# A Restormer block on one core: new due times, GpSimd's results due later, and the weights' preparation moved

## The chip, the cores and the metric

The kernel runs on 1 core of one Trainium2 chip. The metric is device time in microseconds (us). The kernel before takes 4175.92 us (median of 3 runs, 4175.73 to 4176.47). The engines are called PE (matmuls; PEld is its loading of weights), DVE (vector), ACT (activations), POOL (GpSimd) and SP (which only starts DMAs here).

## What is computed

A transformer block on an image batch `x` of 16 x 128 channels x 96 x 96, in float32: channel attention with a residual, then a convolutional feed-forward with a residual.

```
x_hwc = x.transpose(0, 2, 3, 1)
xn1 = _layernorm(x_hwc, ln1_w, ln1_b)
attn_out = _attention(xn1, wq, wk, wv, wp)      # 8 heads, 16 x 16 channel attention per head
x = x + attn_out.transpose(0, 3, 1, 2)
x_hwc = x.transpose(0, 2, 3, 1)
xn2 = _layernorm(x_hwc, ln2_w, ln2_b).transpose(0, 3, 1, 2)
x = x + _ffn(xn2, w_in, w_dw, w_out)            # 1x1 to 512, depthwise 3x3, gelu, 1x1 back to 128
```

In `_attention`, q and k are normalised over the pixels of the image, their product gives a 16 x 16 matrix per head, and its softmax is applied to v. So the first norm and a Gram matrix of a whole image must be finished before the attention's small matrices exist, and these must exist before the second half of the image can begin.

## The kernel before

**Tiling.** An image has 9216 pixels. They are handled in bands of 12 rows (1152 columns of a 128-partition tile), units of 4 rows (384 columns), and quads of 4 blocks of 128 pixels. The hidden 512 channels are four chunks of 128.

**The stages of an image.** First norm ("a"): a band of x is loaded, PE transposes a quad (`forth`, L609), DVE takes its statistics (L616), POOL computes variance plus epsilon (L623) and its power -0.5 (L627), ACT scales the quad into `zT` (L663; DVE does half in the first image, L650), PE accumulates the Gram matrix (L677) and transposes back (`back`, L714), and ACT copies the result into a padded tile `xn` (`place`, L720). Then the attention: about 14 short steps that go back and forth between PE, DVE, POOL and ACT, and end in one 128 x 128 matrix per image. Second norm ("b"): PE multiplies the matrix with `xn` (`mix`, L566), the residual is added (L572, or L575 and a DMA that adds x, L578), and the same steps as in the first norm follow, with a shift by DVE (L631) and ACT's L667 and L718. Feed-forward: PE makes a hidden chunk (L899), ACT copies it to a padded tile (L904), and the depthwise 3 x 3 filter runs in three ways: one chunk of some bands as nine matmuls on PE (L967, gelu at L973); otherwise DVE adds most of the taps (L917), and for two or three taps ACT makes a product (L912) that POOL's DMAs add (L921). Gelu is L925. PE's L990 goes back to 128 channels, DVE adds the residual (L997), SP stores (L1001).

**The order of the work.** `Plan` collects every piece of work with its engine, its cost in ns, a place on a common axis, what it reads and writes, and how long its result takes to reach another engine. `Plan.order` then walks through all of it by a list schedule: an engine that is idle takes the ready piece of the lowest place, buffers are handed out as they come free, and for the pools in `IN_TURN` in the order of places. The place of each kind of work is its position in the image's flow plus an offset from the table `AT` (L33 to L43). A key with `_0` is used for the first image in place of the one without. The result is one fixed order for each engine's queue. The costs in the plan (`T_WEIGHTS`, `T_VARIANCE`, `T_POWER`, `T_ADD`, `T_MOVE`, `SLACK`, `WAIT`) only serve this order; on the chip each engine runs its queue in order and waits for semaphores.

**The start.** POOL clears some tiles and builds `ident`. ACT starts six small DMAs (L276 to L288: norm weights, `wv`, and the depthwise weights `dw`). SP loads the bands of image 0 (L546). In `weights`, `loads` fetches the five larger weights into two tiles borrowed from the pool `h3`, from ACT's queue, with a planned result after `T_WEIGHTS` = 12000 ns. `units` (DVE, L487 to L493) divides the depthwise weights by their first tap, `shifts` (DVE, L478 to L482) prepares the second norm's weight and bias in `w2`, `b2` and the column `none`, and the rest transposes and combines the weights on PE and DVE. `units` and `shifts` read only what the small DMAs bring; `shifts` also gives the token `("w", "shift")` that every `place` reads.

Of the kernel before, what the change touches and what calls it, by code (L numbers as in the profile page):

```python
# [9 lines left out]
F32 = mybir.dt.float32  # L10
# [20 lines left out]
X1_BUFS, XB_BUFS, PR_BUFS, H3_BUFS, ZT_BUFS = 2, 6, 5, 10, 3  # L31
IN_TURN = ("tr", "h3", "pr", "xb", "x1")
AT = dict(  # L33
    load_w=20.7, weights=-42.35, zeros=-138.3, load_a=-151.9, forth_a=0.1, stats_a=-36.15, variance_a=263.5,
    power_a=249.55, scaled_a=74.15, gram=2.55, back_a=-28.75, place_a=112.3, attention=-146.85, mix=-33.95,
    residual=283.8, mixed=-159.7, add_x=-437.65, forth_b=0.35, stats_b=-221.75, variance_b=76.3, power_b=-236.6,
    shift_b=-162.65, scaled_b=19.7, back_b=1.45, place_b=-30.7,
    halo=161.95, hidden=3.15, kept=-18.75, products=83.25, add_last=-139.85, tap=10.15,
    add_first=-120.05, gelu=196.55, conv=2.95, conv_gelu=9.4, out=6.5, add=-10, store=164.8, mix_0=-40.75,
    residual_0=378.9, mixed_0=-198.6, add_x_0=-364.75, gram_0=9.85, forth_a_0=-6.55, forth_b_0=2.65,  # L40
    stats_a_0=-99.05, stats_b_0=-205.9, scaled_a_0=-81.4, scaled_b_0=247.4, back_a_0=-172.15, back_b_0=-50.5,
    place_a_0=-98.9, place_b_0=-35, shift_b_0=-201.25, late=-145.5,
)  # L43
STEP = dict(scaled=0.3, hidden=0.1, products=0.5, tap=0.166, conv=1.6, conv_tap=0.03, out=0.8, out_part=0.05)
SLACK = 300
NORM1_END = 6.0
EARLY = 5
WAIT = dict(POOL=350, SP=1300, ACT=1300)
T_WEIGHTS = 12000
T_VARIANCE = 420  # L50
T_POWER = 1000
T_ADD, T_MOVE = 3060, 1640


class Plan:
# [14 lines left out]
    def op(self, engine, ns, place, work, reads, writes, result, own=None, dma=0, two=False):  # L70

        k = len(self.ops)
        needs = {}
        for t in reads:
            if t in self.writer:
                needs[self.writer[t]] = True  # L80
        for t in writes:
            if t in self.writer:
                needs[self.writer[t]] = True
            for r in self.readers.get(t, ()):
                needs[r] = True
# [12 lines left out]
        self.ops.append((engine, ns, place, work, list(needs), new, result, own or result, dma, two))  # L98
# [111 lines left out]
def tile_restormer_block(  # L210
# [42 lines left out]
    const = ctx.enter_context(tc.tile_pool(name="const", bufs=1))  # L253
# [15 lines left out]
    ones = const.tile([P, 1], F32, name="ones")  # L269
# [17 lines left out]
    per_unit = const.tile([P, NCH], F32, name="per_unit")  # L287
    nc.scalar.dma_start(out=dw, in_=w_dw.rearrange("(n p) o kh kw -> p n (o kh kw)", p=P))  # L288

    wvb = const.tile([P, 1], F32, name="wvb")  # L290
    ccol = const.tile([P, 2, 2], F32, name="ccol")
    ncq = const.tile([1, P], F32, name="ncq")
    none = const.tile([P, 1], F32, name="none")
    wqkT = const.tile([P, 2 * P], F32, name="wqkT")
    cqk = const.tile([1, 2 * P], F32, name="cqk")
    wpT = const.tile([P, P], F32, name="wpT")
# [36 lines left out]
    def z_unit(i, u):  # L333
        k, r = part_of(i, u * UR)
        return ("z", k, r // UR)
# [12 lines left out]
    op = plan.op  # L348

    def at(kind, place, i=1):  # L350
        return place + AT[kind if i else kind + "_0"]
# [25 lines left out]
    def dve(ns, p, f, r, w, two=False):  # L377
        op("DVE", ns, p, f, r, w, ns + 120 + SLACK, ns + 120, two=two)
# [1 line left out]
    def add(p, f, r, w):  # L380
        op("POOL", 950, p, f, r, w, 1400 + SLACK, dma=T_ADD)

    def move(p, f, r, w, ns):
        op("SP", 60, p, f, r, w, 900 + SLACK, dma=ns)

    def act(ns, p, f, r, w):
        op("ACT", ns, p, f, r, w, ns + 150 + SLACK, ns + 150)
# [20 lines left out]
    def weights(p):  # L408

        mine = [("h3", ("weights", k)) for k in range(2)]  # L410
        v, names = staged, iter(range(99))

        def loads():
            a, b = (h3p.tile([P, BR * W], F32, tag="h3", name=f"weights_{k}") for k in range(2))
            v["win"] = a[:, :HID].rearrange("p (n c) -> p n c", c=P)
            v["wout"], v["wp"] = a[:, HID : 2 * HID], a[:, 2 * HID : 2 * HID + P]
            v["wqk"], v["wqkT"] = b[:, : 2 * P], b[:, 2 * P : 4 * P]
            v["wt"] = b[:, 4 * P : 8 * P].rearrange("p (t c) -> p t c", c=P)
            v["centre"], v["w1centre"], v["wvT"] = b[:, 8 * P : 9 * P], b[:, :P], b[:, P : 2 * P]
            nc.scalar.dma_start(out=v["wqk"][:, :P], in_=wq)  # L420
            nc.scalar.dma_start(out=v["wqk"][:, P:], in_=wk)
            nc.scalar.dma_start(out=v["wp"], in_=wp)
            nc.scalar.dma_start(out=v["win"], in_=w_in.rearrange("(n p) c kh kw -> p n (c kh kw)", p=P))
            nc.scalar.dma_start(out=v["wout"], in_=w_out.rearrange("c j kh kw -> c (j kh kw)"))

        def transposed(kind, parts, kept, gives):

# [68 lines left out]
            for n in range(NCH):  # L496
                nc.vector.tensor_scalar(v["wt"][:, n, :], v["win"][:, n, :], unit[:, n : n + 1], None, ALU.mult)

        op("ACT", 400, at("load_w", p), loads, [], mine, T_WEIGHTS, dma=2 * T_MOVE)
        dve(1400, at("weights", p), units, [], [("w", "in")])  # L500
        dve(400, at("weights", p), shifts, [], [("w", "in"), ("w", "conv"), ("w", "shift")])
        transposed(
            "weights", lambda: [v["wqk"][:, :P], v["wqk"][:, P:], v["wp"], wv_sb], keep_qkp, ["qk"]
        )
# [35 lines left out]
    def load(p, i, b):  # L540
        key = x_key(i, b, False)

        def go():
            pool, of = (xpool, xbs) if key == "xb" else (x1pool, x1s)
            of[i, b] = pool.tile([P, BR * W], F32, tag="x", name=f"x_{i}_{b}")
            nc.sync.dma_start(out=of[i, b], in_=x_band(i, b))  # L546

        move(p, go, [], [(key, (i, b), s) for s in range(UPB)], T_MOVE)

    def norm(i, second, place_of):  # L550

        name = f"{'b' if second else 'a'}{i}"
        ab = "_b" if second else "_a"
# [38 lines left out]
        def pixels(s, m):  # L592
# [89 lines left out]
            trs, bt = [(key_, (name, q)) for q in qs], ("batch", (name, m))  # L682
            for q, tr in zip(qs, trs):
                units = {t // TPU: None for t in range(q * QT, (q + 1) * QT)}
                pe(110 * QT, at("forth" + ab, s, i), lambda q=q: forth(q), [xtok(u) for u in units], [tr])
            for j in range(QB * QT // 2):
                dve(341, at("stats" + ab, s, i), lambda j=j: stats(j), [trs[2 * j // QT]], [bt])
            op("POOL", T_VARIANCE, at("variance" + ab, s), variance, [], [bt], T_VARIANCE + 33 + SLACK)
            op("POOL", T_POWER, at("power" + ab, s), power, [], [bt], T_POWER + 33 + SLACK)
            if second:  # L690
                dve(80, at("shift" + ab, s, i), shift, [], [bt])
            for h, (q, tr) in enumerate(zip(qs, trs)):
# [13 lines left out]
        def channels(s, u):  # L706

            d = {}

            def back():  # L710
                d["pB"] = p_bk.tile([P, UT], F32, tag="bk", name=f"pB_{name}_{u}")
                for j in range(TPU):
                    q, k = divmod(u * TPU + j, QT)
                    nc.tensor.transpose(d["pB"][:, j * P : (j + 1) * P], zTs[q][:, k, :P], ident)  # L714

            def place():
                if second:
                    nc.scalar.activation(interior(i, u), rows(d["pB"]), AF.Identity, bias=b2)  # L718
                else:
                    nc.scalar.copy(interior(i, u), rows(d["pB"]))  # L720

            def place_row(k, r, row):
                to = window(xns[k], r, 1, 1)
                nc.scalar.activation(to, rows(d["pB"])[:, row : row + 1, :], AF.Identity, bias=b2)

            copies = []
            if second and u % UPP == 0 and u > 0:
                copies.append((part_of(i, u * UR - 1)[0], PART + 1, 0, UPP))
            if second and u % UPP == UPP - 1 and u < NU - 1:
                copies.append((part_of(i, (u + 1) * UR)[0], 0, UR - 1, -1))  # L730

            pb = ("bk", (name, u))
            quads = {(u * TPU + j) // QT: None for j in range(TPU)}
            pe(110 * TPU, at("back" + ab, s, i), back, [(*zt_of(q), k) for q in quads for k in range(2)], [pb])
            act(t_act(UT, 1) - 43 if second else t_copy(UT), at("place" + ab, s, i), place, [pb, ("w", "shift")], [z_unit(i, u)])
            for k, r, row, of in copies:
                act(225, at("place" + ab, s, i), lambda k=k, r=r, row=row: place_row(k, r, row), [pb, ("w", "shift")], [("z", k, of)])

# [6 lines left out]
        u = 0  # L745
# [272 lines left out]
    jobs, first = [], []  # L1018
# [57 lines left out]
```

## Time and profile before

| what | value |
|---|---|
| median of 3 runs | 4175.92 us |
| the profiled execution | 4175.62 us |
| its span, first to last instruction | 4173.9 us |
| instructions | 52446 |
| mean granted TensorE clock | 0.999 |
| DVE busy | 4070.0 us |
| ACT busy | 3693.7 us |
| POOL busy | 2479.5 us |
| L917, DVE's taps | 2550 instructions, some 1407 ns each |
| L627, POOL's power | 576 instructions, mean 1856 ns (first norm), 1760 ns (second) |
| L623, POOL's variance | 576 instructions, mean 961 and 1020 ns |

A profile here is one execution with its own time; busy time is the time in which an engine has an instruction running, and instructions of PE overlap. "Idle before" an instruction is the time for which its engine had nothing running, with the engine or DMA whose signal ended it. A wait for several signals is put down to the last one. A list of waits gives for each pair the total in us, the number, and the longest. The chain of waits is followed back from the last instruction of the run, at each step to what released it.

### The profile page before, as it was taken

Reading aid. Unit: us, or ns where it says so; the run is one execution under the profiler, and the core shown is the slowest. Engines: PE = TensorE matmul, PEld = TensorE weight load, DVE = VectorE, ACT = ScalarE, POOL = GpSimd, SP = SyncE. Lnnn points to the kernel's source line nnn. Section 1 sums busy time; section 2 is a strip of 40 time slices with the busy share of each in tenths; the row PEclk is TensorE's granted clock in tenths of the full one; section 3 lists DMA queues with packets and bytes.
Section 4 is the critical chain, followed back from the end, with each engine's and each line's share of the span. In section 5 each row is a group of like instructions: output and inputs, shape, how many; then the busy total and the mean of one; then the engine's idle time right before and its main releaser. Section 6 shows DMA issues by size and latency. Waiting matters only on the chain.

```text
span 4173.9 us, 52446 instructions
## 1 busy us (share of the span) xinstructions
PE 4142.5 (99%) x17457; PEld 2679.6 (64%) x17457; DVE 4070.0 (98%) x4676; ACT 3693.7 (88%) x6970; POOL 2479.5 (59%) x2391
## 2 busy tenths in 40 slices
PE   8999999999999999999999999999999999999999
PEld 7666666666666666666666666666666666666565
DVE  6999999999999999999999999999999999999998
ACT  5899989899899989989898898998998999899885
POOL 4656566565665656656576565666756567565442
PEclk9999999999999999999999999999999999999999
DMA  2999999999999999999999998999999999998997
GB/s 88 197 188 215 194 208 208 203 208 197 205 208 201 204 198 212 200 205 211 193 202 205 199 215 185 211 200 209 208 198 202 201 209 201 203 204 184 201 193 159
DMA packets 203935, 827.64 MB, mean 198 GB/s; under 512 B 23568, under 2 KB 24976, under 8 KB 203664
## 3 DMA queue, kind: packets, MB, share of 16 engines
q0 software_dynamic: 164160, 672.47, 83.0%
q1 hardware_dynamic: 37152, 151.01, 9.9%
q8 instruction: 138, 2.26, 0.2%
q10 hardware_dynamic: 2352, 0.81, 0.1%
q14 instruction: 133, 1.09, 0.1%
HBM read 148.26 MB, written 75.50 MB: 54 GB/s over the span
## 4 chain that ended last, share of the span: by engine, by line
PE 88%; DVE 4%; DMA 3%; ACT 3%; POOL 1%; issue 1%; ACTq 0%; POOLq 0%; DVEq 0%
PE h L967 25%; PE h L990 21%; PE h L899 19%; PE g L677 5%; PE h L566 5%; DVE h L917 3%; PE pB_b L714 3%; PE pT_b L609 3%; PE pB_a L714 3%; PE pT_a L609 2%; DMA h<-pr 2%; DMA pr<-pr 1%; ACT pr L912 1%; ACT h L904 0%; DVE st_a L616 0%
## 5 line engine op out<-in xcount | busy, mean ns | idle before, releaser
L917 DVE SCALAR_TENSOR_TENSOR h<-h,ratio,h 128x1152 f32<-128x1152 f32 x2104 | 2915.2, 1407 | 3.6
L912 ACT ACTIVATE pr<-h,ratio 128x1152 f32<-128x1152 f32 x1018 | 1301.6, 1290 | 65.1 <-DMA h<-pr 37.6
L967 PE MATMUL h<-xn,comp 128*128 128x384 f32 x3564 | 1269.3, 485 | 0.0
L990 PE MATMUL h<-h,woutT 128*128 128x384 f32 x3072 | 1137.1, 486 | 1.0 <-ACT h L904 0.4
L899 PE MATMUL h<-xn,winT 128*128 128x384 f32 (+1 forms) x2676 | 1078.6, 500 | 1.1 <-ACT h L904 1.0
L967 PEld LDWEIGHTS h<-xn,comp 128*128 128x128 f32 x3564 | 647.9, 189 | 394.9 <-issue 12.6
L921 POOL DMA_DIRECT2D pr<-pr x573 | 562.6, 989 | 493.2 <-ACT pr L912 385.7
L904 ACT COPY h<-h 128x384 f32<-128x384 f32 (+1 forms) x1338 | 667.9, 520 | 182.0 <-PE h L899 162.1
L990 PEld LDWEIGHTS h<-h,woutT 128*128 128x128 f32 x3072 | 554.2, 190 | 327.2 <-issue 10.3
L921 POOL DMA_DIRECT2D h<-pr x445 | 424.7, 956 | 531.5 <-DVE h L917 119.0
L899 PEld LDWEIGHTS h<-xn,winT 128*128 128x128 f32 x2676 | 475.5, 190 | 269.2 <-issue 39.2
L917 DVE SCALAR_TENSOR_TENSOR h<-h,ratio 128x1152 f32<-128x1152 f32 x446 | 627.3, 1411 | 13.5 <-ACT h L904 5.3
L925 ACT ACTIVATE h<-h 128x1152 f32<-128x1152 f32 x448 | 536.0, 1198 | 17.0 <-DMA h<-pr 13.9
L627 POOL TENSOR_TENSOR rstd_a<-ve_a,mhalf 128x4 f32<-128x4 f32 x288 | 534.4, 1856 | 12.7
L627 POOL TENSOR_TENSOR rstd_b<-ve_b,mhalf 128x4 f32<-128x4 f32 x288 | 506.8, 1760 | 11.3
L667 ACT ACTIVATE zT<-pT_b,nb_b,rstd_b 128x128 f32<-128x128 f32 x1132 | 430.5, 478 | 24.3 <-DVE nb_b L631 21.3
L623 POOL TENSOR_SCALAR ve_b<-st_b 128x4 f32<-128x4 f32 x288 | 293.8, 1020 | 219.8 <-DVE st_b L616 204.8
L623 POOL TENSOR_SCALAR ve_a<-st_a 128x4 f32<-128x4 f32 x288 | 276.8, 961 | 226.0 <-DVE st_a L616 211.8
L663 ACT ACTIVATE zT<-pT_a,rstd_a 128x128 f32<-128x128 f32 x1080 | 316.6, 406 | 19.8 <-POOL rstd_a L627 19.4
L677 PEld LDWEIGHTS g<-zT 128*128 128x128 f32 x2304 | 297.2, 191 | 56.9 <-issue 3.8
L677 PE MATMUL g<-zT 128*128 128x129 f32 x2304 | 305.2, 275 | 0.0
L566 PE MATMUL h<-xn,mwT 128*128 128x384 f32 x768 | 284.3, 490 | 5.6 <-ACT h L904 2.7
(173 smaller groups left out, 3578.6 us busy)
## 6 DMA issues: line engine op xcount, KB each, us to landing
pr<-pr POOLq DMA_DIRECT2D x573, 576.0 KB, 7.3
h<-pr POOLq DMA_DIRECT2D x445, 576.0 KB, 6.9
x<-in_x_dram SPq DMA_DIRECT2D x128, 576.0 KB, 6.2
out_dram<-x SPq DMA_DIRECT2D x127, 576.0 KB, 5.2
x<-in_x_dram POOLq DMA_DIRECT2D x122, 576.0 KB, 6.9
out_dram<-x SPq DMA_DIRECT2D x3, 192.0 KB, 1.9
weights<-in_L_conv_w_in_dram ACTq DMA_DIRECT2D x1, 256.0 KB, 2.9
weights<-in_L_conv_w_out_dram ACTq DMA_DIRECT2D x1, 256.0 KB, 3.0
```

The lines of the kernel that those rows point to most:

```text
L566: nc.tensor.matmul(rows(pm), lhsT=mats[i][0], rhs=interior(i, u), start=True, stop=True)
L623: nc.gpsimd.tensor_scalar(ve, d["mv"][:, :, 2], 1.0 / C, EPS, ALU.mult, ALU.add)
L627: nc.gpsimd.tensor_tensor(rstd, d["ve"], mhalf, ALU.pow)
L677: nc.tensor.matmul(grams[i][:, : P + 1], lhsT=zt[:, :P], rhs=zt, start=(q == 0 and k == 0), stop=(q == NU * TPU // QT - 1 and k == QT - 1),)
L899: nc.tensor.matmul(rows(ph), lhsT=winT[:, n, :], rhs=window(xn, r0 + r, e - r, 1), start=True, stop=True)
L904: nc.scalar.copy(window(h1_, r, e - r, 1), rows(d.pop(("ph", r))))
L912: nc.scalar.activation(to, shifted(t), AF.Copy, scale=ratio[:, n, t : t + 1])
L917: nc.vector.scalar_tensor_tensor(h3, shifted(t), ratio[:, n, t : t + 1], onto, ALU.mult, ALU.add)
L921: nc.gpsimd.dma_start(out=to, in_=d["pr", t], accum_op=ALU.add)
L925: nc.scalar.activation(h3, h3, AF.Gelu)
L967: nc.tensor.matmul(d["pc"], lhsT=comp[:, t, :], rhs=window(xn, r0 + dy, UR, dx), start=(t == 0), stop=(t == 8),)
L990: nc.tensor.matmul(rows(d["po"]), lhsT=woutT[:, n, :], rhs=h3s[g, n][:, s * UR : (s + 1) * UR, :], start=(k == 0), stop=(k == NCH - 1),)
```

## The change

- The table `AT` gets new numbers throughout (all 55 offsets).
- In the plan, the results of POOL's variance and power are taken to arrive 200 and 700 ns later. Nothing in the instructions themselves changes.
- The first load of x is planned with 2300 ns more on SP (`T_START`).
- `loads` issues its five DMAs from SP instead of ACT, with a planned result after 2500 ns instead of 12000 plus the transfer.
- `units` and `shifts` read `mine[:1]`, the first of the two weight tiles, so the plan takes them up only after the loads. No data goes that way.
- A copy of `ones` into `none` is put on ACT's queue right behind its six small DMAs. `shifts` overwrites `none` later.
- `place` of the first norm, which doesn't use `b2`, no longer reads `("w", "shift")`.

```diff
-T_WEIGHTS = 12000
+T_START = 2300
...
+    none = const.tile([P, 1], F32, name="none")
+    nc.scalar.copy(none, ones)
...
-    def move(p, f, r, w, ns):
-        op("SP", 60, p, f, r, w, 900 + SLACK, dma=ns)
+    def move(p, f, r, w, ns, first=0):
+        op("SP", 60 + first, p, f, r, w, 900 + SLACK, dma=ns)
...
-            nc.scalar.dma_start(out=v["wqk"][:, :P], in_=wq)
+            nc.sync.dma_start(out=v["wqk"][:, :P], in_=wq)
...
-        op("ACT", 400, at("load_w", p), loads, [], mine, T_WEIGHTS, dma=2 * T_MOVE)
-        dve(1400, at("weights", p), units, [], [("w", "in")])
-        dve(400, at("weights", p), shifts, [], [("w", "in"), ("w", "conv"), ("w", "shift")])
+        op("SP", 60, at("load_w", p), loads, [], mine, 2500, dma=2 * T_MOVE)
+        dve(1400, at("weights", p), units, mine[:1], [("w", "in")])
+        dve(400, at("weights", p), shifts, mine[:1], [("w", "in"), ("w", "conv"), ("w", "shift")])
...
-        move(p, go, [], [(key, (i, b), s) for s in range(UPB)], T_MOVE)
+        move(p, go, [], [(key, (i, b), s) for s in range(UPB)], T_MOVE, 0 if i or b else T_START)
...
-            op("POOL", T_VARIANCE, at("variance" + ab, s), variance, [], [bt], T_VARIANCE + 33 + SLACK)
-            op("POOL", T_POWER, at("power" + ab, s), power, [], [bt], T_POWER + 33 + SLACK)
+            op("POOL", T_VARIANCE, at("variance" + ab, s), variance, [], [bt], T_VARIANCE + 33 + SLACK + 200)
+            op("POOL", T_POWER, at("power" + ab, s), power, [], [bt], T_POWER + 33 + SLACK + 700)
...
-            act(t_act(UT, 1) - 43 if second else t_copy(UT), at("place" + ab, s, i), place, [pb, ("w", "shift")], [z_unit(i, u)])
+            act(t_act(UT, 1) - 43 if second else t_copy(UT), at("place" + ab, s, i), place, [pb, ("w", "shift")] if second else [pb], [z_unit(i, u)])
```

The offsets of `AT` that the largest groups of work use, before and after:

| key | before | after |
|---|---|---|
| load_w, weights, late | 20.7, -42.35, -145.5 | -10.6, -9.25, 51.6 |
| variance_a, power_a, scaled_a | 263.5, 249.55, 74.15 | 338.3, 317.55, 106.3 |
| variance_b, power_b, shift_b, scaled_b | 76.3, -236.6, -162.65, 19.7 | 95.55, -203.35, -87.55, 78.75 |
| hidden, kept, products, tap, gelu | 3.15, -18.75, 83.25, 10.15, 196.55 | 4.1, -109.5, 36.25, 5.55, 210.35 |
| conv, conv_gelu, out, add | 2.95, 9.4, 6.5, -10 | 3.8, 5.25, 7.35, 0.7 |

More of the change, by code (lines that the diff above doesn't have):

```diff
@@ L33 @@
 AT = dict(
[L34 to L42, printed above, removed]
+    load_w=-10.6, weights=-9.25, zeros=-109.85, load_a=-167.55, forth_a=-12.1, stats_a=-7.7, variance_a=338.3,
+    power_a=317.55, scaled_a=106.3, gram=-0.45, back_a=-56.1, place_a=121.25, attention=-165.9, mix=-18.8,
+    residual=290.95, mixed=-105.85, add_x=-328.55, forth_b=-9.7, stats_b=-262.9, variance_b=95.55,
+    power_b=-203.35, shift_b=-87.55, scaled_b=78.75, back_b=0.45, place_b=-79.8, halo=240.1, hidden=4.1,
+    kept=-109.5, products=36.25, add_last=-62.55, tap=5.55, add_first=-157.75, gelu=210.35, conv=3.8,
+    conv_gelu=5.25, out=7.35, add=0.7, store=226.8, mix_0=-63.1, residual_0=490.65, mixed_0=-265.75,
+    add_x_0=-380.65, gram_0=43.45, forth_a_0=-198.65, forth_b_0=-9.45, stats_a_0=-244.4, stats_b_0=-163.95,
+    scaled_a_0=-13.7, scaled_b_0=305.2, back_a_0=-199.3, back_b_0=-62.8, place_a_0=-193.7, place_b_0=23.1,
+    shift_b_0=-147.65, late=51.6,
 )
@@ L292, in tile_restormer_block @@
     ncq = const.tile([1, P], F32, name="ncq")
-    none = const.tile([P, 1], F32, name="none")
     wqkT = const.tile([P, 2 * P], F32, name="wqkT")
@@ L419, in loads @@
             v["centre"], v["w1centre"], v["wvT"] = b[:, 8 * P : 9 * P], b[:, :P], b[:, P : 2 * P]
-            nc.scalar.dma_start(out=v["wqk"][:, :P], in_=wq)
[L421 to L424, printed above, removed]
+            nc.sync.dma_start(out=v["wqk"][:, :P], in_=wq)
+            nc.sync.dma_start(out=v["wqk"][:, P:], in_=wk)
+            nc.sync.dma_start(out=v["wp"], in_=wp)
+            nc.sync.dma_start(out=v["win"], in_=w_in.rearrange("(n p) c kh kw -> p n (c kh kw)", p=P))
+            nc.sync.dma_start(out=v["wout"], in_=w_out.rearrange("c j kh kw -> c (j kh kw)"))
         def transposed(kind, parts, kept, gives):
```

## The prediction

> **What bounds the kernel now.** I read the page's shares first, then busy time by stretch, the waits, and the timeline of the first 30 us. The columns of the second fence are the stretch, its length, then busy time (and instructions) of PE, PEld, DVE, ACT and POOL, the clock, the DMA share and the rate.
>
> ```profile
> PE 4142.5 (99%) x17457; PEld 2679.6 (64%) x17457; DVE 4070.0 (98%) x4676; ACT 3693.7 (88%) x6970; POOL 2479.5 (59%) x2391
> ```
>
> ```profile
> 0.00:50.00 50.00, 37.72 (x286) 35.90 (x287) 29.05 (x102) 19.22 (x55) 24.42 (x72) 1.00 0.37 123
> 50.00:100.00 50.00, 47.54 (x272) 34.84 (x272) 36.91 (x96) 30.32 (x83) 17.94 (x49) 0.97 0.16 48
> 100.00:200.00 100.00, 94.77 (x396) 60.42 (x395) 98.89 (x103) 87.11 (x165) 60.22 (x55) 0.98 0.92 195
> 200.00:4000.00 3800.00, 3792.14 (x15947) 2447.49 (x15947) 3748.51 (x4234) 3441.84 (x6489) 2320.11 (x2161) 1.00 0.96 203
> ```
>
> PE's idle time is 50 - 37.7 = 12.3 us in the first stretch, 2.5 and 5.2 in the next two, and 7.9 us in the 3800 us after them. The last 174 us hold the rest of 31.4 (4173.9 - 4142.5). A busy PE could still be a waiting one, since ends of matmuls are modelled, so the starts have to be looked at. The chain of waits shows groups of equal matmuls:
>
> ```profile
> 259.12 2.58 PE h L967 x8
> ```
>
> 2.58 / 8 = 0.3225 us each, and the same 2.58 stands for eight of L899 at 1033 and of L990 at 2130 us. The 384-column records are 3564 (L967) + 3072 (L990) + 2236 (L899) + 768 (L566) = 9640, so 3109 us. The 440 wider ones of L899 at 480/384 of that make 177 us. L677 is 2304 x 0.112 (0.89 for 8) = 258 us, and the 128-column transposes of L609 and L714 are 4608 x 0.11 (0.33 for 3) = 507 us. With some 45 us of attention and weights that is about 4096 us of matmul work that the change leaves alone. PE's stream is the bound from 200 us on; DVE, 98% busy, is close behind it. What an order can give back is PE's idle time, and 20.0 of its 31.4 us lie before 200 us.
>
> The Trainium skill (Trainium Kernel Development and Optimization, Performance Expectations) says that matmul busy time is a bad measure of distance to the limit and the share of weight loads a good one. By that, 64% would leave a third of the span, some 1490 us, to be won; by the even 0.3225 us spacing, 8 us after the start.
>
> The first 30 us (start, duration, engine, line, operation, and in brackets the idle time before it):
>
> ```profile
> 5.52 3.65 PE L609 MATMUL h<-ident,x 128*128 128x128 f32 x16 [5.52 <-DMA x<-in_x_dram]
> 7.85 0.17 DVE L487 TENSOR_SCALAR unit<-dw 128x4 f32<-128x4 f32 x1 [6.79 <-DMA dw<-in_L_conv_w_dw_dram]
> 10.26 2.74 DVE L616 BATCH_NORM_STATS2 st_a<-h 128x6 f32<-128x256 f32 x8
> 12.99 0.61 DVE L650 TENSOR_SCALAR zT<-h,rstd_a 128x128 f32<-128x128 f32 x2
> 13.71 1.28 ACT L663 ACT_TABLE_LOAD   x1 [13.71 <-DVE zT L650]
> 15.42 0.47 PE L714 MATMUL pB_a<-ident,zT 128*128 128x128 f32 x1 [1.29 <-ACT zT L663]
> 23.56 0.52 ACTq L424 DMA_DIRECT2D weights<-in_L_conv_w_out_dram  x1
> 24.13 0.63 ACT L663 ACTIVATE zT<-h,rstd_a 128x128 f32<-128x128 f32 x2 [1.93 <-DMA weights<-in_L_conv_wk_dram]
> 25.62 0.63 PE L609 MATMUL h<-ident,x 128*128 128x128 f32 x4 [0.95 <-DVE zT L650]
> ```
>
> DVE waits for the small dw load, prepares the depthwise weights (7.85 to 10.26), and only then takes the statistics of tokens that PE had transposed from 6.6 us on. ACT loads its table only when the first zT is due. At 21.7 us it issues five weight loads.
>
> **Part 1, DVE starts with the statistics.** L487 to L493 and L478 to L482 leave the head of DVE's queue. Sixteen transposes take 3.65 us, 0.21 each, so quad 0 is done at 5.52 + 4 x 0.21 + 0.2 = 6.6 and quad 1 at 7.4. Four statistics at 0.34 (2.74 / 8) end the first quad's at 8.1. In the trace POOL's variance and power and the next zT follow that point by 1.7 us (11.28 to 12.99), which gives 9.8; but DVE has four more statistics first, whose tokens are there at 9.2, so zT starts at 10.2 in place of 12.99. ACT has its table by then, because the copy of `none` puts the 1.28 us load right behind its first DMA issues, under the 5.5 us in which everybody waits for x. PE's third transpose back then comes at about 11.2 (two DVE scalings to 10.8, two transposes) in place of 15.42: -4.2 us. Bounds: -2.8 (DVE's step alone) and -5.5 (both waits that the waits list for L714 here, 4.2 on DVE and 1.3 on ACT).
>
> On the array's clock: L677's eight records at 19.59 us take 1.54 us, at 28.58 us 1.06; PE is cold until about 21 us. I let the cold stretch move with the work: 0. The Trainium skill (TensorE: Matmul & The Clock Gate, What's actually happening) gives a window of about 3.4 us whose activity sets the clock; the gap of 4.2 us is longer than that, the 1.4 to 2 us left would not be, so by the page the clock might rise some 5 us earlier and save half of that, about 2.7 us more.
>
> **Part 2, weight loads from SP.** The five issues on ACT, 21.72 to 24.13, cost PE 0.95 + 0.29 us at 25.6 and 27.8: -1.3 (bounds 0 and -1.3). On SP they stand behind the eight loads of image 0 and ahead of image 1's first band; that band needs a buffer which PE frees with the last quads of image 0, near 38 us, so 0. If that cover were gone, five issues at 0.45 would be 2.2 us late at a load for which PE waits 0.2 us now. They are wanted at 42.6 (L435) and land in some 3 us.
>
> **Part 3, where the preparation goes.** The written order has it between the statistics of quads 9 and 12: 1.65 us (7.85 to 9.50) and 0.9 us (9.41 to 10.34). Behind it in DVE's queue wait the scalings of quads 8 to 10, then ACT and PE's gram. A quad takes DVE 0.75 + 0.61 = 1.36 us and PE 1.66, so DVE has 0.3 spare each. The nearest row is the 1.6 us of L441 to L446 at 43.4, after which PE idled 0.17 + 0.44: +0.8 for 2.55 us, bounds 0 and +2.55.
>
> **Part 4, the new due times.** In the written order, with these durations, the PE work ahead of the first tap (L917) falls from 70.1 to 68.1 us, and DVE's from 53.9 to 53.2. If that stretch stays bound by PE it is worth 2.0, if not 0: I take -1.0. The DVE-bound stretch from 129 to 186 us then starts earlier as a whole.
>
> **Part 5, POOL later.** DVE's work between a quad's last statistic and its shift rises from 4.45 to 5.78 us (median of 288), against 1.02 + 1.76 us on POOL (means of L623 and L627) plus its queue. That removes most of
>
> ```profile
> DVE nb_b L631 <- POOL rstd_b L627: 22.7, 22, 2.8
> ACT zT L663 <- POOL rstd_a L627: 19.4, 32, 1.3
> ```
>
> (total, times, longest). DVE and ACT have that time to spare: PE's idle time from 200 to 4000 us is only 7.9. So -1.0, bounds 0 and -7.9; what it could cost is the second rival.
>
> Sum: -4.2 - 1.3 + 0.8 - 1.0 - 1.0 = -6.7. The profiled execution took 4175.6 (1.7 around its span of 4173.9), 0.3 under the median of 4175.9. So 4168.9 there and **4169 us** as a median. By the lower bounds -5.5 - 1.3 - 2.0 - 7.9 = -16.7, by the upper -2.8 + 2.55 = -0.25: 4159 to 4176 for this case.
>
> **Rivals.**
> 1. *More than the start is won.* The stalls of 50 to 200 us (2.5 + 5.2) halve and the 7.9 us behind them go: a further -3.9 and -6.9, 4158. For it: both engines that feed PE wait for POOL today. Against: PE there waits mostly single microseconds for ACT copies (L566 for L904 2.7 us in four waits), not for POOL.
> 2. *Slower: token buffers held too long.* A PSUM bank of `tr` is held from a quad's transposes to its last scaling, 10.1 us in the median of the timeline; with 1.3 us more, the next transposes on it come late and PE, in order, waits. It decides where a bank's spare time until its reuse is below 1.3 us (median 1.7; under 0.5 us in 7% of quads). 7% of 576 is 40 quads, at half of 1.3 us each +26: 4195. Against: 576 quads in 4080 us want a bank each 14.2 us, and 10.1 + 1.7 + 1.3 = 13.1 still fits.
> 3. *Swallowed.* The attention of image 0 or the DVE-bound stretch (DVE 98.9 of 100 us busy) keeps its place in time, and PE idles longer before it: 4175. Against: the chain of waits runs unbroken from the first statistics through attention into that stretch.
>
> **How the numbers follow.** 0.2% is 8.4 us, about what can be told from no change: below 4167.6 is faster, above 4184.3 slower. The forecast has 0.50, with 0.14 of it below 4167.6; rival 1 has 0.24, rival 2 0.17, rival 3 0.09. So faster 0.38, within 0.36 + 0.09 = 0.45, slower 0.17. The range runs from rival 1 down by a little, 4157, to 4187, which leaves out most of rival 2.
>
> **What would show it.** Right: first zT on DVE near 10 us, the table load before 6, no ACT gap at 22 to 24, PE idle in the first 50 us near 7 in place of 12.3, first tap some 6 us earlier, idle time of L631 for POOL below 10 us, and PE idle from 200 to 4000 still near 8. Wrong: PE idle there above 20, with L609 or L714 waiting for scalings of zT; or a first stretch that gains and a second that gives it back.

## The result, and the profile after

The changed kernel takes 4163.86 us (median of 10 runs, 4160.99 to 4166.25) against 4175.5 us for the kernel before, run beside it (10 runs, 4169.46 to 4177.61): the ratio is 0.9975, 95% interval 0.9967 to 0.9982. In a later set it was 0.9982 (0.9973 to 0.9990), 4164.32 against 4173.03 us. By these ratios it is faster by 7.5 to 10.4 us (the medians differ by 8.7 and 11.6): a gain of 0.2%, but both intervals lie below 1. The profiled execution took 4165.01 us, with a span of 4163.3 us, 10.6 us shorter than the one before. In code and profiles of the changed kernel the lines named here that stand behind L291 have a number two higher than before (L609 is L611, L917 is L919).

The engines' busy time in the page of the changed kernel:

```profile
PE 4138.0 (99%) x17457; PEld 2680.2 (64%) x17457; DVE 4072.3 (98%) x4676; ACT 3690.1 (89%) x6971; POOL 2439.2 (59%) x2391
```

Its windows by stage (start and end, length, then busy time of PE, PEld, DVE, ACT and POOL, the granted clock, DMA share and GB/s):

```profile
0.00:50.00 50.00, 42.46 (x322) 38.91 (x323) 31.84 (x114) 21.77 (x61) 23.88 (x78) 0.96 0.37 123
50.00:100.00 50.00, 47.34 (x262) 35.09 (x261) 39.53 (x89) 34.34 (x86) 22.37 (x44) 0.97 0.25 72
100.00:200.00 100.00, 96.41 (x419) 62.76 (x418) 99.06 (x108) 91.97 (x175) 66.93 (x60) 1.00 0.93 192
200.00:4000.00 3800.00, 3792.14 (x15938) 2448.96 (x15937) 3754.87 (x4234) 3436.10 (x6487) 2281.93 (x2163) 1.00 0.96 203
```

PE's idle time in the first 50 us falls from 12.3 to 7.5 us, and from 100 to 200 us from 5.2 to 3.6. In the 3800 us behind them PE is busy for 3792.14 us, as before. That the last digit agrees is chance: in profiles of kernels that differ from the changed one only at the start, or not at all, the same number goes from 3787.16 (e10_warm) to 3795.29 us (e11_warm2). So a gain of the new order in the steady stages can't be seen on PE here.

The first 17 us in the timeline of the changed kernel:

```profile
3.92 1.28 ACT L291 ACT_TABLE_LOAD   x1 [3.92 <-issue]
5.17 3.65 PE L611 MATMUL h<-ident,x 128*128 128x128 f32 x16 [5.17 <-DMA x<-in_x_dram]
6.30 0.43 DVE L618 BATCH_NORM_STATS2 st_a<-h 128x6 f32<-128x256 f32 x1 [5.25 <-PE h L611]
9.87 1.29 DVE L652 TENSOR_SCALAR zT<-h,rstd_a 128x128 f32<-128x128 f32 x4
10.26 0.59 PE L716 MATMUL pB_a<-ident,zT 128*128 128x128 f32 x2 [1.44 <-DVE zT L652]
...
11.01 0.33 PE L716 MATMUL pB_a<-ident,zT 128*128 128x128 f32 x1 [0.16 <-ACT zT L665]
...
11.76 1.50 PE L679 MATMUL g<-zT 128*128 128x129 f32 x8
14.55 1.58 PE L679 MATMUL g<-zT 128*128 128x129 f32 x8
16.73 1.06 PE L679 MATMUL g<-zT 128*128 128x129 f32 x8
```

The table is loaded while everybody waits for x, DVE's first work of the norm is at 6.30 (10.26 before), and the third transpose back at 11.01 (15.42 before). The groups of eight of L679 are still slow twice, and at full speed from 16 us on (from 21 us before). The first such group of the kernel before:

```profile
16.59 1.93 PE L677 MATMUL g<-zT 128*128 128x129 f32 x8
```

The waits for POOL's power in the changed kernel (total, times, longest):

```profile
ACT zT L665 <- POOL rstd_a L629: 6.4, 5, 1.6
DVE nb_b L633 <- POOL rstd_b L629: 3.6, 5, 0.9
```

They fall from 42.1 to 10.0 us in all, as the later arrival planned for POOL's results intends, while PE's idle time from 200 to 4000 us stays at 7.9.

How far the start reaches is read from single instructions in the traces (us from the span's start):

| kernel | first zT on DVE | third transpose back | 33rd transpose of tokens | first tap | last matmul of the output convolution |
|---|---|---|---|---|---|
| before | 12.99 | 15.42 | 25.6 | 95.3 | 4169.9 |
| changed | 9.87 | 11.01 | 19.3 | 88.2 | 4159.2 |
| difference | -3.1 | -4.4 | -6.3 | -7.1 | -10.7 |

A first tap that comes 7.1 us earlier isn't yet 7.1 us won, because the new order also puts some 1.7 us of PE's work behind it. What is won or lost is better read from the starts of PE's matmuls. I add up by how much each next one starts later than the median spacing for its kind in these two traces:

| stretch, us | before | changed | difference |
|---|---|---|---|
| before the first matmul | 5.5 | 5.2 | -0.3 |
| from there to 100 | 18.8 | 13.7 | -5.1 |
| 100 to 200 | 10.0 | 5.6 | -4.4 |
| from 200 on | 25.0 | 24.2 | -0.8 |

So half of the 10.7 us is won before 100 us and most of the rest between 100 and 200, where the idle time of PE shows only 1.6 of it.

### The profile page after: what moved, and what is told of

Same layout as the page of the kernel before. It is cut to its first block, busy times and chain, and to the rows that moved or that the text cites. A ratio compares the mean times of both kernels' runs of the same rounds, so it can differ in the third digit from the quotient of the medians.

```text
span 4163.3 us, 52440 instructions
## 1 busy us (share of the span) xinstructions
PE 4138.0 (99%) x17457; PEld 2680.2 (64%) x17457; DVE 4072.3 (98%) x4676; ACT 3690.1 (89%) x6971; POOL 2439.2 (59%) x2391
## 4 chain that ended last, share of the span: by engine, by line
PE 91%; DVE 3%; ACT 3%; DMA 1%; issue 1%; POOL 1%; ACTq 0%; POOLq 0%; DVEq 0%
PE h L969 25%; PE h L992 22%; PE h L901 20%; PE h L568 6%; PE g L679 6%; PE pB_a L716 3%; PE pB_b L716 3%; PE pT_b L611 3%; PE pT_a L611 3%; DVE h L919 2%; DMA h<-pr 1%; ACT pr L914 1%; ACT zT L669 0%; ACT h L906 0%; ACT h L927 0%
## 5 line engine op out<-in xcount | busy, mean ns | idle before, releaser
L919 DVE SCALAR_TENSOR_TENSOR h<-h,ratio,h 128x1152 f32<-128x1152 f32 x2104 | 2913.0, 1405 | 4.2
L901 PE MATMUL h<-xn,winT 128*128 128x384 f32 (+1 forms) x2676 | 1064.7, 500 | 3.7 <-ACT h L906 2.7
L969 PEld LDWEIGHTS h<-xn,comp 128*128 128x128 f32 x3564 | 646.3, 189 | 390.5 <-issue 12.3
L923 POOL DMA_DIRECT2D pr<-pr x573 | 576.0, 1018 | 456.7 <-ACT pr L914 329.0
L923 POOL DMA_DIRECT2D h<-pr x445 | 415.0, 933 | 500.9 <-DVE h L919 126.6
L919 DVE SCALAR_TENSOR_TENSOR h<-h,ratio 128x1152 f32<-128x1152 f32 x446 | 626.2, 1408 | 14.9 <-ACT h L906 8.4
L629 POOL TENSOR_TENSOR rstd_a<-ve_a,mhalf 128x4 f32<-128x4 f32 x288 | 511.3, 1776 | 11.4 <-POOL ve_a L625 0.2
L625 POOL TENSOR_SCALAR ve_a<-st_a 128x4 f32<-128x4 f32 x288 | 293.9, 1021 | 230.5 <-DVE st_a L618 199.7
L625 POOL TENSOR_SCALAR ve_b<-st_b 128x4 f32<-128x4 f32 x288 | 269.3, 935 | 257.0 <-DVE st_b L618 231.0
L679 PEld LDWEIGHTS g<-zT 128*128 128x128 f32 x2304 | 293.3, 191 | 44.7 <-issue 2.1
L679 PE MATMUL g<-zT 128*128 128x129 f32 x2304 | 304.7, 275 | 0.0
L720 ACT ACTIVATE xn<-pB_b,b 128x384 f32<-128x384 f32 x384 | 244.2, 636 | 59.2 <-PE pB_b L716 58.6
```

Source lines behind the costliest of these rows:

```text
L625: nc.gpsimd.tensor_scalar(ve, d["mv"][:, :, 2], 1.0 / C, EPS, ALU.mult, ALU.add)
L629: nc.gpsimd.tensor_tensor(rstd, d["ve"], mhalf, ALU.pow)
L679: nc.tensor.matmul(grams[i][:, : P + 1], lhsT=zt[:, :P], rhs=zt, start=(q == 0 and k == 0), stop=(q == NU * TPU // QT - 1 and k == QT - 1),)
L901: nc.tensor.matmul(rows(ph), lhsT=winT[:, n, :], rhs=window(xn, r0 + r, e - r, 1), start=True, stop=True)
L919: nc.vector.scalar_tensor_tensor(h3, shifted(t), ratio[:, n, t : t + 1], onto, ALU.mult, ALU.add)
L923: nc.gpsimd.dma_start(out=to, in_=d["pr", t], accum_op=ALU.add)
```

## The experiments

Twelve runs were made in three sets, each set on one chip beside the kernel before (4176.21, 4172.10 and 4173.03 us in the median). Ratios, not times, are compared across sets. One profiled execution can lie several us from its kernel's median, as will be seen; where both are given, the ratio is the verdict and the trace tells where the time went.

**Preparation back at the head of DVE's queue (e1_head).**

```diff
+        staged["head"] = [units, shifts]
-        for work in plan.order():
+        head = staged.pop("head")
+        for work in head + [w for w in plan.order() if w not in head]:
             work()
```

> The changed kernel with the depthwise preparation (units, then shifts: L489 to L495 and L480 to L484) put back at the head of DVE's queue; every other instruction keeps its order, the table load stays early and the big weights stay on SP. Theory S (the start wins it: DVE's first statistics and all that follows them come earlier, and this shift is passed on to the end): DVE starts its statistics at 10.3 in place of 6.3 us, the first zT comes at 13.0 in place of 9.9, some 0.9 us of PE waits at 26 to 33 us go away again, the first tap (L919) is at 90 to 91 in place of 88.1, and the time is 2 to 3 us above the changed kernel's 4163.9: 4166 to 4167. Theory R (the re-planned order, POOL's later due times among it, wins it in the steady flow): the first tap is late too, but the time stays at 4164. Theory W (a later stretch bound by another engine swallows the start): first tap late, time 4164, and the PE idle time from 100 to 200 us falls by the same 2 to 3 us.

Measured: 4171.56 us, ratio 0.9989 (0.9980 to 0.9998); 3 to 6 us of the gain are lost. PE's timeline:

```profile
13.40 1.22 PE L717 MATMUL pB_a<-ident,zT 128*128 128x128 f32 x3 [4.20 <-DVE zT L653]
...
15.32 1.93 PE L680 MATMUL g<-zT 128*128 128x129 f32 x8
```

PE's wait of 4.20 us for DVE's first zT is back (1.44 in the changed kernel), and with it a longer stretch of slow matmuls. The first tap is at 91.4 us, 3.2 us later. In the trace theory S holds. In time it is favoured, with a loss of its 2 to 3 us or more where R and W expected none, but its interval overlaps those of the changed kernel.

**The table load late (e2_table).**

```diff
-    nc.scalar.copy(none, ones)
```

> The changed kernel without the early copy of none (L291), so that ACT loads its function table when the first zT is due. Theory S: the 1.28 us of the load lie between DVE's first zT and ACT's, PE's third transpose back is at 12.3 in place of 11.0, the first tap at 89.4 in place of 88.1, time 4165.2. Theory R and theory W: time 4164, with the first tap at 89.4 all the same.

Measured: 4167.26 us, ratio 0.9983 (0.9974 to 0.9992). ACT and PE in the timeline:

```profile
10.50 1.28 ACT L665 ACT_TABLE_LOAD   x1 [10.50 <-DVE zT L652]
...
12.22 0.48 PE L716 MATMUL pB_a<-ident,zT 128*128 128x128 f32 x1 [1.44 <-ACT zT L665]
```

The wait is there with the size given, 1.28 us more in front of the third transpose back. But the first tap is at 88.2 us, as in the changed kernel's profile, and the ratio lies beside that kernel's second one (0.9982). The 33rd transpose is only 0.8 us later than there (20.0), because this execution has fewer slow matmuls (one group of eight at 1.83 us, then 1.06), and from 50 to 100 us its clock reads 1.00 in place of 0.97. For the time this run is inconclusive: an effect of 1.3 us is smaller than what the clock does from one execution to the next.

**The weight loads on ACT (e3_actload).**

```diff
-            nc.sync.dma_start(out=v["wqk"][:, :P], in_=wq)
+            nc.scalar.dma_start(out=v["wqk"][:, :P], in_=wq)
```

and so for the other four.

> The changed kernel with the five big weight loads issued by ACT in place of SP, where the new order has them (behind the scalings of the first four quads). Theory S: ACT issues 2.3 us of loads between 12 and 15 us, the transposes back and the gram behind it come later by 1 to 2.3 us, the first tap is at 89 to 90.4 and the time at 4165 to 4166.2. Theory R and theory W: 4164.

Measured: 4168.87 us, ratio 0.9995 (0.9986 to 1.0004). In the trace ACT issues the loads at 14.4 to 18.1 us, PE's busy time from 15 to 20 us falls from 5.00 to 4.41 us, and the first tap is at 88.3, 0.1 us later than in the changed kernel's profile and 2.4 later than in its second one (after_again, below). Against the first profile a part is hidden, since the clock reads 1.00 from 50 to 100 us here and 0.97 there. The median loses 5 us or more, which the trace (the fastest of its 11 runs) doesn't show. That the loads cost something on ACT is supported; where the rest of the loss lies stays open.

**All three undone: only the new order is left (e4_all_three).** The three edits above together.

> The changed kernel with all three edits of the start undone (depthwise preparation at the head of DVE's queue, table load late, the five big weight loads issued by ACT where the new order has them, behind the first three quads' scalings); what is left of the change is its re-planned order. Theory S: the first zT is at 13.0, the losses of +2.2, +1.3 and +1.3 to 2.4 us add up, the first tap is at 93 to 94 us and the time at 4169 to 4170; the last 5 to 6 us to the kernel before belong to the new order. Theory R: 4164 to 4166. Theory W: 4164, with less PE idle time from 100 to 200 us.

Measured: 4173.58 us, ratio 0.9993 (0.9984 to 1.0002). First zT at 13.1, first tap at 94.1, where S had 93 to 94; before it was 95.3. The re-planned order without the three edits isn't told from no change, so R's 4164 to 4166 falls. The median is some 4 us above what S expected; S gave the new order 5 to 6 us, and the runs give it 2.9 (from 6.7 to -0.8). The trace says where it helps: by the spacing of PE's starts the stretch from 100 to 200 us loses 5.5 us, against 10.0 before.

**Only the three edits, in the order of before (e5_start_only).** The early copy of `none`, the loads on SP, and:

```diff
+        if (kind, count[kind]) == ("stats", 21):
+            staged["late"][0]()
+        if (kind, count[kind]) == ("scaled", 10):
+            staged["late"][1]()
...
         for work in plan.order():
-            work()
+            if work not in staged["late"]:
+                work()
```

> The kernel before with its own order, due times and POOL results, and only the three edits of the start: the table load early, the five big weight loads issued by SP, the depthwise preparation moved from the head of DVE's queue to behind the 21st statistic (units) and the 10th pair of scalings of zT (shifts). Theory S: the first zT is at 10, the first tap at 95.3 - 4.2 - 1.3 + 0.8 = 90.6 us, and the time 4175.5 - 4.7 = 4170.8, perhaps 2 us less where the clock rises earlier with it. Theory R: 4175 to 4176. Theory W: first tap at 90.6, time 4175.

Measured: 4169.2 us, ratio 0.9987 (0.9978 to 0.9995), so 5.4 us (2.1 to 9.2). The first tap is at 86.8 us, 8.5 us earlier than before; the last matmul of the output convolution is 7.4 us earlier. So a shift at the start does go through to the end, and W, which wanted the same tap and no gain in time, falls with R. The first tap is 3.8 us earlier than the 90.6 that S summed without the clock. PE's timeline says where from:

```profile
12.12 1.06 PE L686 MATMUL g<-zT 128*128 128x129 f32 x8
```

The first group of eight is already at full speed (1.93 us before, 1.50 in the changed kernel). A part of the 3.8 us is luck further on: from 50 to 100 us the clock reads 0.97 in the profile of the kernel before and 1.00 here, which is 3.4 us at half the clock that this execution was spared. By the spacing of PE's starts 8.5 us are won ahead of 100 us, 0.6 from 100 to 200, and 1.7 are lost behind.

**POOL's later results alone, in the kernel before (e8_pool_only).**

```diff
-            op("POOL", T_VARIANCE, at("variance" + ab, s), variance, [], [bt], T_VARIANCE + 33 + SLACK)
-            op("POOL", T_POWER, at("power" + ab, s), power, [], [bt], T_POWER + 33 + SLACK)
+            op("POOL", T_VARIANCE, at("variance" + ab, s), variance, [], [bt], T_VARIANCE + 33 + SLACK + 200)
+            op("POOL", T_POWER, at("power" + ab, s), power, [], [bt], T_POWER + 33 + SLACK + 700)
```

> The kernel before with only the later results of POOL (the further 200 and 700 ns) and its order computed anew from them. Theory S: DVE's waits for POOL (L631 for L627, 22.7 us) shrink below 10 us, PE's idle time from 200 to 4000 us stays at 7 to 10, the first tap at 95 and the time at 4174 to 4177. Theory R: 4165 to 4170. A third outcome, if later results hold token buffers longer: 4178 or more.

Measured: 4179.24 us, ratio 1.0017 (1.0008 to 1.0026): 7.1 us slower. Its waits for POOL, then its steady stages:

```profile
ACT zT L663 <- POOL rstd_a L627: 12.2, 14, 3.6
DVE nb_b L631 <- POOL rstd_b L627: 5.4, 7, 1.0
```

```profile
200.00:4000.00 3800.00, 3786.75 (x15925) 2447.73 (x15924) 3749.92 (x4230) 3429.71 (x6480) 2326.73 (x2160) 1.00 0.95 202
```

The waits shrink as intended (42.1 to 17.6 us), and PE's idle time rises from 7.9 to 13.2 us. Less waiting on POOL, more on PE, in one and the same order. It is the third outcome. A token bank is indeed held longer, for 10.8 in place of 10.0 us in the median, but the changed kernel holds it for 11.5 without such a loss, so this alone isn't the cause. The idle time of a single profile is weak evidence too (12.8 us in e10_warm's, whose order is the changed kernel's); that the run is slower rests on its eleven times. The longest of its PE waits are single ones of 0.8 to 1.4 us for scalings, copies and loads of x.

**POOL's results as before, in the changed kernel (e6_no_pool).** The same edit backwards, the order computed anew.

> The changed kernel with the results of POOL's variance and power counted as before (without the further 200 and 700 ns), the order computed anew. Theory S: the start is the same, DVE's and ACT's waits for POOL come back (L633 for L629 above 15 us in all), and since PE does not see them the time stays within 2 us of 4163.9 and PE's idle time from 200 to 4000 us at 7 to 10. Theory R (POOL's later results win in the steady flow): 4168 or more, with PE idle there above 12 us.

Measured: 4183.29 us (8 runs), ratio 1.0026 (1.0016 to 1.0036), some 18 to 21 us slower than the changed kernel. The first tap is at 89.5; PE's idle time from 200 to 4000 us is 15.4 us. S expected no loss here and is wrong; by its numbers this run speaks for R. One of the places, in the timelines of ACT and PE:

```profile
3533.18 1.25 ACT L914 ACTIVATE pr<-h,ratio 128x1152 f32<-128x1152 f32 x1 [4.17 <-DMA h<-pr]
3534.34 0.24 ACT L803 COPY wide<-g 128x128 f32<-128x128 f32 x1
...
3535.24 0.38 PE L815 MATMUL g<-gs,wqkT 128*128 128x1 f32 x2 [2.71 <-DVE wide L808]
```

and its windows there:

```profile
3530.00:3540.00 10.00, 7.29 (x26) 4.55 (x25) 5.90 (x12) 3.76 (x8) 4.36 (x5) 0.82 0.86 160
3540.00:3550.00 10.00, 10.00 (x30) 5.71 (x29) 8.60 (x10) 8.12 (x15) 2.60 (x3) 0.84 0.87 180
```

ACT's queue stands 4.17 us before a product of the depthwise convolution whose buffer a DMA hasn't finished. The two small copies of the next image's attention are behind it, DVE waits for these, PE for DVE: 2.7 us. After the stall the granted clock is lower for a while: 0.82 and 0.84 in the mean of these two stretches of 10 us are 3.6 + 3.2 = 6.8 us at half the clock, which cost up to 3.4 us more. By the spacing of PE's starts this profile loses 36.9 us from 200 us on, 12.7 more than the changed kernel's; this place is some 6 of them, and the others weren't followed.

**The old due times with all other edits (e7_old_at).** `AT` as before, the rest as in the changed kernel.

> The changed kernel with the due times (AT) of the kernel before, all other edits kept, the order computed anew. Theory S in its narrow form (only the three edits of the start count): 4164 to 4166, first tap 88 to 89.5. If the new due times carry part of it (the wider form of S: a better order from 40 to 200 us): first tap at 89 to 91 and 4166 to 4169. Theory R: 4170 or more, with the loss between 200 and 4000 us.

Measured: 4172.67 us, ratio 1.0002 (0.9993 to 1.0011). The first zT is at 9.6, but the first tap at 98.8, 10.6 us later than in the changed kernel; from 200 to 4000 us PE is idle for 7.5 us, about as little as in the kernel before. The loss is in the attention of image 0:

```profile
55.00:60.00 5.00, 3.03 (x21) 2.48 (x21) 1.06 (x6) 0.85 (x2) 0.69 (x1) 0.94 0.57 159
60.00:65.00 5.00, 2.34 (x9) 1.67 (x8) 2.45 (x8) 0.89 (x4) 2.33 (x4) 0.50 0.19 77
65.00:70.00 5.00, 5.00 (x14) 3.18 (x13) 1.29 (x3) 2.16 (x9) 0.00 (x0) 0.53 0.00 0
```

PE waits there for a load of x and for DVE's softmax (2.31 us before L861), and then works at half the clock. So the start's gain was made and then lost again before the first tap. In an order that is computed with the other edits, the new due times are needed to keep it; e5_start_only keeps it in the order of before, with the three edits put in by hand. That is more than either form of S allowed; R's place for the loss, the steady stages, is wrong.

**The changed kernel again, and a warm PE (after_again, e10_warm, e11_warm2, e12_warm_split).** The clock had come up in e2 and e5, so the last set went to it. e10_warm adds, ahead of `ident`:

```diff
+    idle = const.tile([P, P], F32, name="idle")
+    nc.vector.memset(idle, 0.0)
+    for k in range(17):
+        nc.tensor.matmul(banks[3][:, :P], lhsT=idle, rhs=idle, start=True, stop=True)
```

e11_warm2 also puts 12 such matmuls into a free part of `gram`'s bank behind quad 3's transposes; e12_warm_split takes e11 with 13 in place of 17, and loads the first band of x in three pieces.

> The changed kernel once more, beside the kernel before on the chip of the next three. All theories: 0.9967 to 0.9982 of the kernel before, the profile as it was but for the stretch of slow matmuls at 12 to 16 us, which by the theory of the clock (the array's clock is raised or dropped by what PE did in a window before) may come or not.

> The changed kernel with 17 matmuls of zeros (128x128, into the PSUM bank that quad 3 fills later) on PE from about 1.3 us, while everybody waits for x. Theory of the clock: the 16 transposes of quads 0 to 3 take some 1.9 in place of 3.65 us, DVE's first zT comes at 9.1 in place of 9.9, the slow L679 at 12 to 16 us (1.50 and 1.58 us for eight, against 1.06 later) may be gone, the first tap is at 85.5 to 87.5 in place of 88.1 and the time 0.8 to 2.6 us below the changed kernel's. Rival (the slow start of PE is not the clock but the data's way into it, or zeros do not count): transposes at 3.65 us, no gain.

> As the one before, with 12 more matmuls of zeros behind quad 3's transposes, so that PE is not idle before the first transposes back. Theory of the clock: from 5.2 us on no slow matmul at all, L679's eights at 1.06 us from the first, first tap at 85 to 86.5, time 1.5 to 3 us below the changed kernel's. Rival: the further matmuls only delay the first transposes back (to 11 to 11.5 us where the clock stays low): 0 to 1 us slower than the changed kernel.

> As the one before, with the first band of x loaded in three pieces of 192 KB and 13 in place of 17 matmuls of zeros ahead. If the first tokens land earlier in the smaller pieces (4 to 4.5 in place of 5.2 us), DVE starts that much earlier and the first tap and the time fall by a further 0.7 to 1.2 us; if the landing is set by the fixed part of a transfer and by the loads issued with it, there is no change, or up to 0.9 us of loss from two more issues ahead of the second band.

Measured: after_again 0.9982 (0.9973 to 0.9990), e10_warm 0.9996 (0.9987 to 1.0005), e11_warm2 0.9980 (0.9971 to 0.9989), e12_warm_split 0.9977 (0.9968 to 0.9986).

The same program twice, first the windows of the first profile, then those of the second:

```profile
10.00:15.00 5.00, 4.58 (x25) 4.16 (x26) 2.65 (x9) 3.15 (x10) 3.98 (x7) 0.72 1.01 407
15.00:20.00 5.00, 5.00 (x44) 5.00 (x44) 3.70 (x13) 1.96 (x6) 2.29 (x5) 0.94 0.62 207
```

```profile
10.00:15.00 5.00, 4.43 (x35) 4.01 (x36) 3.59 (x13) 3.16 (x10) 4.15 (x7) 1.00 1.01 406
15.00:20.00 5.00, 5.00 (x48) 5.00 (x47) 3.60 (x12) 3.10 (x9) 3.70 (x7) 1.00 0.68 222
```

With the same instructions in the same order, the clock drops in one execution and not in the other. The first tap is at 88.2 in the one and 86.0 in the other, the span 4163.3 and 4161.1 us.

e10_warm in PE's timeline:

```profile
1.11 6.05 PE L268 MATMUL h<-idle 128*128 128x128 f32 x34 [1.11 <-DVE idle L266]
7.00 1.91 PE L615 MATMUL h<-ident,x 128*128 128x128 f32 x16
10.89 0.59 PE L720 MATMUL pB_a<-ident,zT 128*128 128x128 f32 x2 [1.98 <-DVE zT L656]
...
12.60 1.93 PE L683 MATMUL g<-zT 128*128 128x129 f32 x8
```

The 16 transposes take 1.91 in place of 3.65 us, as the theory of the clock had it: zeros count. But the 17 matmuls are 34 records and end at 7.0 us, 1.8 us after x has landed; and in the gap before 10.89 the clock is lost again, for the stretch in which it was meant to help. The first tap is at 90.8 us in place of the 85.5 to 87.5 expected. No gain: the ratio is 0.14% worse than that of the changed kernel beside it. e11_warm2 fills that gap:

```profile
8.45 2.84 PE L619 MATMUL g<-idle 128*128 128x128 f32 x24
...
12.09 1.06 PE L687 MATMUL g<-zT 128*128 128x129 f32 x8
```

From 6.7 to 45 us no slow matmul is left, though x is taken up 1.4 us late. But the first tap is at 88.4 us, not at the 85 to 86.5 expected: the clock drops later, in the attention of image 0 (0.94 from 50 to 100 us). Its time can't be told from that of the changed kernel, nor can e12's (first tap 89.1). In e12 the first of the three pieces of x lands at 3.8 us, 1.4 us before the whole band in e11, so smaller pieces do land earlier. But the zeros end at 6.8 us as well, so this had no way to show, and what the split load is worth stays open.

## Why the prediction was right, and where it was wrong

The sign and the range hold; 4163.9 lies 5 us below the 4169 of the forecast. The range of 30 us is wide, and 4163.9 lies below the bound of 4167.6, to which the prediction gave 0.38. That the sum comes near is partly luck: two of its terms aren't found where they were put, and two gains weren't in it.

- *Part 1, DVE starts with the statistics: -4.2.* Right. First zT at 9.87 (10.2), third transpose back at 11.01 (about 11.2): -4.4. e1_head puts its larger share back (zT at 13.0), e2_table shows the table's 1.28 us.
- *The cold stretch: 0.* This term was mis-sized. From the start to the 33rd transpose the changed kernel gains 6.3 us; 4.4 are part 1 and 0.95 the wait for ACT's load issues, so 1.0 is left for the clock. In after_again the 33rd transpose is at 17.8, 7.8 earlier, and in e5_start_only at 18.0, 7.6 earlier; part 1 is 4.3 and 4.1 there, and 2.6 us are left in both. So 1.0 us in one execution and 2.6 in two others, in place of 0. The slow group that the prediction puts at 19.59 us starts at 19.80; nothing rests on it. The prediction's estimate from the Trainium skill's window (TensorE: Matmul & The Clock Gate, What's actually happening) was 2.7 us, and the runs agree with it better than with the assumption that the cold stretch just moves along.
- *Part 2, loads from SP: -1.3.* The gap of ACT at 22 to 24 us is gone, with PE's 0.95 us behind it. In the changed order they would cost 0.1 to 2.4 us at the first tap (e3_actload, against the two profiles of the changed kernel), by that run's median more, for which no place was found.
- *Part 3, the preparation's new place: +0.8.* PE's starts have gaps of 0.2, 0.2 and 0.4 us at 26, 30 and 33 us, behind units and shifts. Right.
- *Part 4, new due times: -1.0.* A gain of the due times is there, but not where the prediction put it. PE's work ahead of the first tap does fall, by 1.7 us, and the first tap is 1.2 us earlier in e4_all_three than before; but this work is done behind the tap, and by the spacing of PE's starts nothing is won ahead of it (e4 loses 19.4 us ahead of 100 us, the kernel before 18.8). The gain lies in the stretch that the prediction let start "earlier as a whole", for nothing: from 100 to 200 us PE loses 4.5 to 7.0 us in the ten profiles with the new due times and 9.2 to 10.0 in the four with the old ones (before, e5, e7, e8). These four all have a drop of the clock there (0.97 or 0.98); the five new ones that have one too lose 6.3 to 7.0, so some 3 us are the order's. And without the new due times the other edits lose 10.6 us before the first tap (e7_old_at), for which the sum had no term.
- *Part 5, POOL later: -1.0.* Wrong. The step that failed is the price itself: from "DVE and ACT have that time to spare" a small gain and a bound of 0 above were taken. The waits went as said, but alone the edit costs 7.1 us (e8_pool_only), outside its bounds, and to take it out of the changed kernel costs 18 to 21 (e6_no_pool). It has no price of its own: the due times and the results' times give an order together. Which wait makes e8 slower stays open.

In the profiles, with 10.7 us in place of the sum's 6.7, PE wins 5.4 us ahead of 100 us in place of 5.7 (parts 1 to 4), 4.4 between 100 and 200 in place of nothing, and 0.8 behind in place of 1.0 (part 5). The missing 4 us thus lie between 100 and 200 us: some 3 of order, and the rest the drop of the clock that the kernel before has there (0.98) and the changed one hasn't (1.00). Ahead of 100 us the unpriced clock made up for part 4. Rival 1 asked for half of the idle time of 50 to 200 us (7.7 before, 6.3 in the changed kernel) and for all of the 7.9 us behind 200, which didn't come (7.9 us in both profiles). Rival 2's mechanism is visible, since a token bank is held for 11.5 in place of 10.0 us in the median, but PE's steady idle time stayed, so it didn't decide. Rival 3 is refuted by e5_start_only, whose 8.5 us at the first tap are still 7.4 at the end. By the three edits alone the kernel gains 5.4 us (2.1 to 9.2), and undoing them in the changed kernel costs 5 to 8 (0.9993 against 0.9975 and 0.9982). So by the middle values the start is more than half of the gain. The new order gives the rest; its runs alone (e4_all_three) can't be told from no change, and that it helps is read from the traces between 100 and 200 us.

## What to carry to other kernels

Where one engine is busy for 99.8% of the steady stages, look for the gain in the stretches before they begin: of 8.5 us saved here ahead of the first tap, 7.4 came out at the end (e5_start_only). An instruction that comes earlier is a gain only if no work was moved behind it. A long list of waits on engines that aren't the bound (42 us here) is no reserve, and shortening it can make the bound wait more. In an order that is computed from many numbers, no number can be priced alone: with one of them taken back, a kernel that gained 0.2% lost 0.3%, so such numbers are to be tried in sets and judged by the runs.

## What the hardware showed unexpectedly

PE's clock can differ between two executions of one program, and with it the time: the 2.2 us between the first taps of the changed kernel's two profiles are also the difference of their spans. How much of the whole scatter (4157.33 to 4170.85 us in after_again) it explains wasn't shown. Drops come in portions: 0.72 and 0.94 over two windows of 5 us (changed kernel) are 2.8 + 0.6 = 3.4 us at half the clock; 0.82 and 0.84 over two of 10 us (e6_no_pool) are 3.6 + 3.2 = 6.8, twice that; 0.94, 0.50 and 0.53 (e7_old_at) are 0.6 + 5.0 + 4.7 = 10.3, three times that. The Trainium skill (TensorE: Matmul & The Clock Gate, What's actually happening) says that the window of 3.4 us runs freely and doesn't begin with the kernel. That fits two executions of one program of which only one drops. A stall of some 2 to 3 us on PE can therefore cost up to 1.7 us more for each portion behind it (one in e10_warm after 1.98 us, two in e6_no_pool after 2.71), and whether it does is partly luck.

The clock's column doesn't show the cold start: it reads 1.00 from 5 to 10 us, where 16 transposes take 3.65 us, and 1.91 once PE was busy before. The durations have to be read there.

The loads on SP landed later than the 3 us or so assumed: those of `wq` and `wk`, issued at 8.9 and 9.4 us behind eight bands of x, took 8.3 and 7.9 us, and the three behind them were issued only from 16.9 us on. They are wanted at 36.9 (L437), so it cost nothing.
